# Keys stored once and read in two pieces, SyncE in program order, scales loaded later: a fused attention and feed-forward kernel on one core

## The chip, the core and the metric

The kernel runs on one core of a Trainium2 chip. A core has five engines with queues of their own: TensorE (PE, with its weight loads shown as PEld), VectorE (DVE), ScalarE (ACT), GpSimd (POOL) and SyncE (SP), which here does nothing but issue transfers. 16 DMA engines move data between DRAM and the on-chip memory. Transfers issued by SP are queue q1 of the profile, those of POOL q0, those of ACT q10. The metric is the device time of one execution in microseconds (us); the time of a kernel is the median of its runs.

## The reference

One sequence of 4096 tokens of 256 features goes through causal attention with 16 heads of 16 features, a layer norm, a gated feed-forward network and a second layer norm, all in float32.

```python
xn  = layernorm(x) * gamma + beta
q, k, v = split(xn @ w_qkv.T)                 # 16 heads of 16
sim = causal(q * 16**-0.5 @ k.T)
x   = layernorm(x + softmax(sim) @ v)
h   = silu((x @ w1.T) * s1) * ((x @ w2.T) * s2)     # 1024 wide
h   = gelu((h @ h1.T) * hs1)
h   = gelu((h @ h2.T) * hs2)
out = layernorm(x + (h @ w3.T) * s3)
```

The weights w1, w2, h1, h2 and w3 are small whole numbers (ternary times 8), and each comes with a vector of scales for its outputs.

## The kernel before

**Accuracy by parts.** [...] So Q and K are split into a high part (rounded) and a low part (what is left), and the score is the sum of three products: high by high, high by low, low by high. This is done in one matmul by stacking rows: a K tile has, for each head, 16 rows of high parts, 16 of high parts again, 16 of low parts and 2 rows of ones (KR = 50 rows); a Q tile has 16 rows of high, 16 of low and 16 of high parts, and 2 rows that receive the negated row maximum, itself split in two.

**Blocks and stages.** Tokens are cut into 8 blocks of 512. `projections` (L200 to L293) normalizes a block, transposes it, multiplies it with the weights of K, Q and V, splits K and Q into kh and kl, and stores them in DRAM tensors `kaug`, `qaug` and `vaug`, one of each per block. Per block and per K or Q there are six stores of 256 KB (L269), because the high part is stored twice; in block 0 they go in turn over the queues of ACT, SP and POOL, later all over POOL's. The rows of ones are stored by SP (L274).

**Attention** (`layer`, L296 on) runs 32 steps, one for each block of queries (in the order 0, 1, 2, 3, 4, 6, 7, 5) and each of four groups of 4 heads. Two streams run side by side, and the emission order of the program interleaves them:

- `row_max` (L425 to L473) loads the Q tile qt of the step (two loads of 48 rows, L429), and for each key block up to the query block takes a K tile mk, multiplies (L442), masks the diagonal block (L449) and reduces to row maxima on DVE (L453). At the end the maxima are transposed, negated, split, and written by four small SP transfers (L469, qt<-hl) into the last two rows of qt.
- `scores` (L476 to L498) takes a K tile sk of its own, multiplies again with rows and columns exchanged (L486), and takes the exponential on ACT (L490). `product` (L500) multiplies with the V tile vk into opsum (L504), some units later.

The row-maximum stream runs ahead of the scores by one step and some units. `fetch` (L401 to L421) loads K tiles for both streams: at the start of tile j it issues the load of tile j+1, in two halves (two heads in partitions 0 on, two in partitions 64 on, L410); for sk the V tile follows (L416). mk, sk and vk have two buffers each, qt four. There are 144 mk tiles and 144 sk tiles.

**Feed-forward** (`feed`, from L729) takes a finished block of 512 tokens; its matmuls are dealt out in pieces between the units of attention, so that PE always has work. Its weights are loaded by POOL (L665), 22 tiles of 512 KB for each block. `start` (L675) loads x and the stored attention output `at`, and adds them in `total`. The last block in the order is done by `closing` after attention has ended, and `inspect` (L707) compares the weights with their rounded values on DVE, through mk buffers, near the end.

**Scales.** `scales` (L117) loads four scale vectors in an element by element layout and one broadcast row, and computes w1_half and w12 from them on POOL. It is called in `layer` just before attention begins.

**Order.** PE, DVE, ACT and POOL execute in the order in which the program emits (`in_order`, L63). DMA instructions are left out of that rule, so that a scheduler places them, SP's whole queue among them: it puts the loads of x and of the scales at the front of SP's queue, and loads qt several steps ahead where a buffer is free. An instruction on SP whose buffer or data is not there yet holds up all that stand behind it.

```python
if i.engine in engines and "DMA" not in type(i).__name__:
```

Of the kernel before, what the change touches and what calls it, by code (L numbers as in the profile page):

```python
# [7 lines left out]
F32 = mybir.dt.float32  # L8
FR = mybir.dt.float32r
AF = mybir.ActivationFunctionType  # L10
ALU = mybir.AluOpType
# [4 lines left out]
N, E, H, D = 4096, 256, 16, 16  # L16
# [4 lines left out]
B = 512  # L21
NB = N // B
NQ = H // 4
KR = 50
# [10 lines left out]
ORDER = (0, 1, 2, 3, 4, 6, 7, 5)  # L35
# [12 lines left out]
class Layer:  # L48
# [13 lines left out]
    @contextmanager  # L62
    def in_order(self, *engines):  # L63

        block = self.nc.cur_bb.bb
        start = len(block.instructions)
        yield
        last = {}
        for i in block.instructions[start:]:
            if i.engine in engines and "DMA" not in type(i).__name__:  # L70
                if i.engine in last:
                    self.after(i, last[i.engine])
                last[i.engine] = i.name
# [8 lines left out]
    def run(self):  # L82
        tc, nc, a = self.tc, self.nc, self.a
        with ExitStack() as ctx:
            dram = self.pool(ctx, "dram", space=DRAM)
            cst = self.pool(ctx, "cst")
            self.small = self.pool(ctx, "small", 4)
            self.qaug = [dram.tile([H, 48, B], F32, name=f"qaug{b}") for b in range(NB)]
            self.kaug = [dram.tile([H, KR, B], F32, name=f"kaug{b}") for b in range(NB)]
            self.vaug = [dram.tile([NQ, P, 4, 4, D + 1], F32, name=f"vaug{b}") for b in range(NB)]  # L90
            self.attn = [dram.tile([B, E], F32, name=f"attn{b}") for b in range(NB)]

            self.ident = cst.tile([P, P], F32, name="ident")
            make_identity(nc, self.ident)
            self.mhalf = cst.tile([P, 4], F32, name="mhalf")
            nc.gpsimd.memset(self.mhalf, -0.5)
            self.wbad = cst.tile([P, 22], F32, name="wbad")
            self.wseq = (
                [("glu", g, 0) for g in range(4)]
                + [(n, g, k) for n in ("h1T", "h2T") for g in range(4) for k in range(2)]  # L100
                + [("w3T", 0, k) for k in range(2)]
            )
            self.sc = {}
            for n in ("w1_s", "w2_s", "h1_s", "h2_s"):
                self.sc[n] = cst.tile([P, 8], F32, name=n)
            self.w1_half = cst.tile([P, 8], F32, name="w1_half")
            self.w12 = cst.tile([P, 8], F32, name="w12")
            self.s3 = cst.tile([P, E], F32, name="s3")

            own = mybir.EngineType  # L110
            with ExitStack() as fctx, self.in_order(own.PE, own.DVE, own.Activation, own.Pool):
                self.layer(fctx)
            bad = self.verdict(cst)
            with tc.If(bad > 0), ExitStack() as gctx:
                self.general(gctx)

    def scales(self):  # L117
        for n, t in self.sc.items():
            self.nc.sync.dma_start(t, self.a[n].rearrange("(c p) -> p c", p=P))
        self.nc.gpsimd.tensor_scalar(self.w1_half, self.sc["w1_s"], 0.5, None, ALU.mult)  # L120
        self.nc.gpsimd.tensor_tensor(self.w12, self.w1_half, self.sc["w2_s"], ALU.mult)
        s3 = self.a["w3_s"].rearrange("(o f) -> o f", o=1)
        self.nc.sync.dma_start(self.s3, s3.broadcast_to([P, E]))

# [75 lines left out]
    def projections(self, ctx):  # L200
# [4 lines left out]
        nc, a, ps = self.nc, self.a, self.ps  # L205
# [46 lines left out]
        for b in range(NB):  # L252
            xh, xl = parts.pop(b)
            prods = [(wh, xh, c) for c in range(2)] + [(wl, xh, c) for c in range(2)] + [(wh, xl, c) for c in range(2)]
            for off, dst, order in ((E, self.kaug, (0, 0, 1)), (0, self.qaug, (0, 1, 0))):
                kp = ps.tile([P, 2, B], F32, name="s", tag="s", bufs=3)
                for T in range(2):
                    for n, (wp, xp, c) in enumerate(prods):
                        nc.tensor.matmul(
                            kp[:, T], wp[:, c, off + T * P : off + (T + 1) * P], xp[:, c], start=n == 0, stop=n == 5  # L260
                        )
                kh = wk.tile([P, 2, B], FR, name="kh")
                nc.scalar.copy(kh, kp)
                kl = wk.tile([P, 2, B], FR, name="kl")
                nc.vector.tensor_tensor(kl, kp, kh.bitcast(F32), ALU.subtract)
                for n, (i, g) in enumerate(sorted((i, g) for g, i in enumerate(order))):
                    for T in range(2):
                        queues = (nc.scalar, nc.sync, nc.gpsimd) if b == 0 else (nc.gpsimd,)
                        queues[(2 * n + T) % len(queues)].dma_start(  # L269
                            dst[b][8 * T : 8 * T + 8, 16 * g : 16 * g + 16, :], (kh, kl)[i][:, T].bitcast(F32)  # L270
                        )
                yield 12 * MM, True
                if dst is self.kaug:
                    nc.sync.dma_start(self.kaug[b][:, 48:KR, :], ones)  # L274
                    if b + 1 < NB:
                        yield from front(b + 1, xb)
                        if b + 2 < NB:
                            xb = fetch(b + 2)
            if b + 2 < NB:
                self.layernorm(xb, xb)  # L280
            v = vst[b % 2]
            vps = ps.tile([P, 4, E], F32, name="s", tag="s", bufs=3)
            for t in range(4):
                for n, (wp, xp, c) in enumerate(prods):
                    nc.tensor.matmul(
                        vps[:, t], xp[:, c, t * P : (t + 1) * P], wp[:, c, 2 * E :], start=n == 0, stop=n == 5
                    )
            for t in range(4):
                nc.scalar.copy(v[:, :, t, :, 0:D], vps[:, t].rearrange("p (q h d) -> p q h d", q=NQ, d=D))
            nc.gpsimd.dma_start(  # L290
                self.vaug[b].rearrange("q p t h d -> p q (t h d)"), v.rearrange("p q t h d -> p q (t h d)")
            )
            self.projected = b  # L293
            yield 12 * MM, True

    def layer(self, ctx):  # L296
# [7 lines left out]
        nc = self.nc  # L304
# [65 lines left out]
        half = P // 2  # L370
# [18 lines left out]
        nc.vector.tensor_copy(tri, tri_f)  # L389
        opsum = ps.tile([P, B], F32, name="opsum")  # L390
        nc.vector.memset(opsum, 0.0)
        self.scales()

        steps = [(qb, qd) for qb in ORDER for qd in range(NQ)]
        order = {
# [5 lines left out]
        def fetch(kind, key):  # L401

            seq = order[kind]
            j = seq.index(key)
            while loaded[kind] < min(j + 2, len(seq)) and seq[loaded[kind]][2] <= self.projected:
                qb, qd, kb = nxt = seq[loaded[kind]]
                kt = (mk if kind == "m" else sk).tile([P, 2, B], FR, name=kind + "k")
                for e in range(2):
                    hs = slice(4 * qd + e, 4 * qd + 4, 2)
                    nc.sync.dma_start(  # L410
                        kt[half * e : half * e + KR].bitcast(F32), self.kaug[kb][hs].rearrange("r p t -> p r t")
                    )
                vt = None
                if kind == "s":
                    vt = sk.tile([P, 4, 4, D + 1], F32, name="vk")
                    nc.sync.dma_start(  # L416
                        vt.rearrange("p t h d -> p (t h d)"), self.vaug[kb][qd].rearrange("p t h d -> p (t h d)")
                    )
                tiles[kind, nxt] = kt, vt
                loaded[kind] += 1  # L420
            return tiles[kind, key]  # L421
# [3 lines left out]
        def row_max(qb, qd):  # L425
            qt = qtile[qb, qd] = qp.tile([P, 2, B], FR, name="qt")
            for e in range(2):
                hs = slice(4 * qd + e, 4 * qd + 4, 2)
                nc.sync.dma_start(  # L429
                    qt[half * e : half * e + 48].bitcast(F32), self.qaug[qb][hs].rearrange("r p t -> p r t")  # L430
                )
            mp = small.tile([P, 2, 2, 4, NB], F32, name="mp")
            nc.gpsimd.memset(mp, NEG)
            for kb in range(qb + 1):
# [240 lines left out]
    def start(self, b):  # L675

        nc = self.nc
        self.busy.add("at")
        x1 = self.load(b)
        at = self.fk.tile([P, 4, E], F32, name="at")  # L680
        nc.sync.dma_start(at, tokens(self.attn[b]))

        def total():
            nc.gpsimd.tensor_tensor(x1, x1, at, ALU.add)
            self.free("at")

        self.defer("next", total, 7)
        for delay, step in self.norm_steps(x1, x1):
            self.defer("next", step, delay)
        return x1  # L690
# [383 lines left out]
```

## Time and profile before

| what | value |
|---|---|
| median of 3 runs | 2522.06 us (2519.75 to 2528.87) |
| the profiled execution, its own time | 2522.7 us |
| its span | 2521.0 us |
| mean granted TensorE clock | 0.926 |
| 0 to 240 us: PE busy, DMA share | 163.57 us, 0.69 |
| 240 to 2220 us: PE busy, DMA share | 1876.24 us, 0.47 |
| 2340 to 2521 us: PE busy, DMA share | 107.89 us, 0.34 |
| moved in all | 310.02 MB in 251,811 packets |
| L453, row maxima on DVE | 1152 instructions, 1132 ns each |
| L490, exponentials on ACT | 1152 instructions, 954 ns each |

The first row maximum starts at about 66 us, the last score at 2347 us; before that stretch lies the projection of the first two blocks, after it the last feed-forward block. "DMA share" is the mean busy share of the 16 DMA engines. A row such as "mk<-kaug SPq DMA_DIRECT2D x288, 200.0 KB" says that SP issued 288 transfers of 200 KB from kaug into mk; an mk tile takes two of them. In the waits, "PE s L486 <- DMA qt<-hl: 12.9, 4, 4.7" says that PE's instructions of line 486 waited 12.9 us in all, 4 times, 4.7 us at the longest, until that transfer had landed.

### The profile page before, as it was taken

Reading aid. Unit: us, or ns where it says so; the run is one execution under the profiler, and the core shown is the slowest. Engines: PE = TensorE matmul, PEld = TensorE weight load, DVE = VectorE, ACT = ScalarE, POOL = GpSimd, SP = SyncE. Lnnn points to the kernel's source line nnn. Section 1 sums busy time; section 2 is a strip of 40 time slices with the busy share of each in tenths; the row PEclk is TensorE's granted clock in tenths of the full one; section 3 lists DMA queues with packets and bytes.
Section 4 is the critical chain, followed back from the end, with each engine's and each line's share of the span. In section 5 each row is a group of like instructions: output and inputs, shape, how many; then the busy total and the mean of one; then the engine's idle time right before and its main releaser. Section 6 shows DMA issues by size and latency. Waiting matters only on the chain. (4 is left out here: it accounts for less than half of the span.)

```text
span 2521.0 us, 36370 instructions
## 1 busy us (share of the span) xinstructions
PE 2258.4 (90%) x13986; PEld 1216.5 (48%) x13986; DVE 1563.3 (62%) x1826; ACT 1393.1 (55%) x1698; POOL 705.8 (28%) x1021
## 2 busy tenths in 40 slices
PE   4768999999998999999999999999999999999458
PEld 3545444545454544544455435554455434544246
DVE  3445687675657576676756686666765577662353
ACT  2233555645655666556656655666666676567311
POOL 2333323242313052312404142323204222132201
PEclk8688889979999989999999989998999999999779
DMA  6776834525453544444444535463355343447333
GB/s 189 190 183 160 188 104 112 133 78 125 108 130 98 142 104 116 108 127 119 114 115 120 132 83 134 98 146 93 100 130 140 98 125 89 108 108 197 93 98 85
DMA packets 251811, 310.02 MB, mean 123 GB/s; under 512 B 41328, under 2 KB 179696, under 8 KB 251632
## 3 DMA queue, kind: packets, MB, share of 16 engines
q1 hardware_dynamic: 141920, 184.87, 26.2%
q0 software_dynamic: 108352, 120.91, 21.8%
q8 instruction: 113, 1.85, 0.3%
q10 hardware_dynamic: 1360, 1.84, 0.2%
q14 instruction: 66, 0.54, 0.1%
HBM read 268.45 MB, written 38.54 MB: 122 GB/s over the span
## 5 line engine op out<-in xcount | busy, mean ns | idle before, releaser
L453 DVE TENSOR_REDUCE mp<-s 128x2 f32<-128x1024 f32 (+3 forms) x1152 | 1265.0, 1132 | 562.8 <-PE s L442 406.1
L490 ACT ACTIVATE p<-s 128x1024 f32<-128x1024 f32 (+3 forms) x1152 | 1062.2, 954 | 672.2 <-PE s L486 658.9
L486 PE MATMUL s<-qt,sk 50*128 50x512 f32 (+3 forms) x2304 | 513.5, 452 | 85.0 <-DVE mp L453 49.5
L442 PE MATMUL s<-mk,qt 48*128 48x512 f32 (+3 forms) x2304 | 512.2, 446 | 55.5 <-DVE mp L453 19.3
L504 PE MATMUL opsum<-p,vk 128*17 128x512 f32 (+3 forms) x4608 | 558.0, 586 | 1.2 <-POOL p L493 1.0
L823 PE MATMUL m<-act,wt 128*128 128x512 f32 x1792 | 477.2, 409 | 0.7 <-DVE xl L778 0.7
L486 PEld LDWEIGHTS s<-qt,sk 50*128 50x128 f32 x2304 | 222.1, 192 | 398.9 <-DVE mp L453 145.2
L823 PEld LDWEIGHTS m<-act,wt 128*128 128x128 f32 x1792 | 321.9, 189 | 123.7 <-issue 53.0
L442 PEld LDWEIGHTS s<-mk,qt 48*128 48x128 f32 x2304 | 229.0, 196 | 305.0 <-ACT p L490 134.0
L504 PEld LDWEIGHTS opsum<-p,vk 128*17 128x17 f32 x4608 | 97.6, 98 | 232.9 <-issue 213.2
L493 POOL TENSOR_SCALAR_AFFINE_SELECT p<-p 128x256 f32<-128x256 f32 x256 | 102.2, 409 | 293.9 <-ACT p L490 292.9
L665 POOL DMA_DIRECT2D wt<-h1T_in x64 | 48.9, 764 | 425.0 <-PE m L823 230.9
L665 POOL DMA_DIRECT2D wt<-h2T_in x64 | 48.6, 759 | 366.5 <-PE m L823 311.5
L748 POOL TENSOR_TENSOR act<-raw,act 128x512 fp32r<-128x512 f32 x112 | 143.0, 1277 | 8.9
L831 ACT ACTIVATE raw<-m,h_s 128x512 f32<-128x512 f32 x112 | 77.1, 688 | 107.6 <-PE m L823 107.6
L795 PE MATMUL m<-xh,wt 128*128 128x512 f32 x224 | 104.9, 468 | 12.4 <-DVE th L799 9.5
L449 PEld LDWEIGHTS s<-tri,pick 64*128 64x128 f32 x1024 | 96.5, 205 | 8.1 <-DVE tri L389 1.2
L795 PE MATMUL m<-xl,wt 128*128 128x512 f32 x224 | 92.4, 413 | 0.0
L449 PE MATMUL s<-tri,pick 64*128 64x128 f32 (+1 forms) x1024 | 88.6, 252 | 1.0 <-DVE tri L389 1.0
L747 POOL CAST act<-raw 128x512 fp32r<-128x512 f32 x112 | 68.2, 609 | 42.4 <-ACT raw L752 42.4
L747 POOL CAST act<-th 128x512 fp32r<-128x512 f32 x56 | 34.4, 614 | 144.9 <-DVE th L801 144.6
L748 POOL TENSOR_TENSOR act<-th,act 128x512 fp32r<-128x512 f32 x56 | 71.5, 1277 | 4.7
(126 smaller groups left out, 1496.3 us busy)
## 6 DMA issues: line engine op xcount, KB each, us to landing
mk<-kaug SPq DMA_DIRECT2D x288, 200.0 KB
sk<-kaug SPq DMA_DIRECT2D x288, 200.0 KB
wt<-h1T_in POOLq DMA_DIRECT2D x64, 512.0 KB, 4.2
wt<-h2T_in POOLq DMA_DIRECT2D x64, 512.0 KB, 4.1
vk<-vaug SPq DMA_DIRECT2D x144, 136.0 KB
qt<-qaug SPq DMA_DIRECT2D x64, 192.0 KB
wt<-w1T_in POOLq DMA_DIRECT2D x34, 256.0 KB, 3.8
wt<-w2T_in POOLq DMA_DIRECT2D x34, 256.0 KB, 5.1
```

The costliest lines, as they stand in the source:

```text
L442: nc.tensor.matmul(m[:, e, :k1], qt[rows, r, t * P : (t + 1) * P], kt[rows, r, :k1], start=True, stop=kb != qb,)
L449: nc.tensor.matmul(m[:, e, k1 - P + half * i : k1], pick[rows, i], tri[rows, : P - half * i], start=False, stop=i == 1,)
L453: nc.vector.tensor_reduce(mp[:, r, :, t, kb], m[:, :, :k1], AX.X, ALU.max)
L486: nc.tensor.matmul(s[:, e, lo:], kt[rows, r, t * P : (t + 1) * P], qt[rows, r, lo:], start=True, stop=True)
L490: nc.scalar.activation(p[:, :, lo:], s[:, :, lo:], AF.Exp, scale=0.25)
L493: nc.gpsimd.affine_select(out=p[:, :, lo : lo + P], in_=p[:, :, lo : lo + P], compare_op=ALU.is_ge, fill=0.0, base=0, pattern=[[0, 2], [1, ...
L504: nc.tensor.matmul(opsum[32 * j : 32 * j + D + 1, lo:], vt[:, t, j], pt[j // 2][:, j % 2, lo:], start=first, stop=last,)
L665: self.nc.gpsimd.dma_start(dst, src)
L747: nc.gpsimd.tensor_copy(hi, src)
L748: nc.gpsimd.tensor_tensor(lo, src, hi.bitcast(F32), ALU.subtract)
L795: nc.tensor.matmul(s, wt[:, 2 * i + k, cols], x[:, k], start=k == n == 0, stop=k == n == 1)
L823: nc.tensor.matmul(s, wts[k // 4][:, k % 4, cols], x[:, k % 4], start=k == n == 0, stop=k == 7 and n == 1)
```

## The change

Three edits are made together.

1. `kaug` is stored as 16 high rows, 16 low rows and 2 rows of ones (34 rows for each head instead of 50), `qaug` as 16 high and 16 low rows (32 instead of 48). The stores per block and tensor fall from six to four. The tiles in on-chip memory are unchanged. Each half of a K tile is now loaded in two pieces: 16 rows (the high part) and then 34 rows (high, low, ones); each half of a Q tile as 32 rows and then 16 rows. A new method `rows` issues one piece.
2. SP's instructions, DMA instructions included, are put under the rule of program order.
3. `scales` is called at the first `start`, and w1_half and w12 are computed in that block's `total`.

```diff
-            if i.engine in engines and "DMA" not in type(i).__name__:
+            if i.engine in engines and (i.engine == mybir.EngineType.SP or "DMA" not in type(i).__name__):
...
-            self.qaug = [dram.tile([H, 48, B], F32, name=f"qaug{b}") for b in range(NB)]
-            self.kaug = [dram.tile([H, KR, B], F32, name=f"kaug{b}") for b in range(NB)]
+            self.qaug = [dram.tile([H, 32, B], F32, name=f"qaug{b}") for b in range(NB)]
+            self.kaug = [dram.tile([H, 34, B], F32, name=f"kaug{b}") for b in range(NB)]
...
-            with ExitStack() as fctx, self.in_order(own.PE, own.DVE, own.Activation, own.Pool):
+            with ExitStack() as fctx, self.in_order(own.PE, own.DVE, own.Activation, own.Pool, own.SP):
...
+    def rows(self, dst, first, src):
+        n = src.shape[1]
+        self.nc.sync.dma_start(dst[first : first + n].bitcast(F32), src.rearrange("r p t -> p r t"))
...
-                for n, (i, g) in enumerate(sorted((i, g) for g, i in enumerate(order))):
+                for i, part in enumerate((kh, kl)):
                     for T in range(2):
...
-                            dst[b][8 * T : 8 * T + 8, 16 * g : 16 * g + 16, :], (kh, kl)[i][:, T].bitcast(F32)
+                            dst[b][8 * T : 8 * T + 8, 16 * i : 16 * i + 16, :], part[:, T].bitcast(F32)
...
-                    nc.sync.dma_start(self.kaug[b][:, 48:KR, :], ones)
+                    nc.sync.dma_start(self.kaug[b][:, 32:34, :], ones)
...
-        self.scales()
...
                 for e in range(2):
                     hs = slice(4 * qd + e, 4 * qd + 4, 2)
-                    nc.sync.dma_start(
-                        kt[half * e : half * e + KR].bitcast(F32), self.kaug[kb][hs].rearrange("r p t -> p r t")
-                    )
+                    self.rows(kt, half * e, self.kaug[kb][hs, 0:16])
+                    self.rows(kt, half * e + 16, self.kaug[kb][hs])
...
-                nc.sync.dma_start(
-                    qt[half * e : half * e + 48].bitcast(F32), self.qaug[qb][hs].rearrange("r p t -> p r t")
-                )
+                self.rows(qt, half * e, self.qaug[qb][hs])
+                self.rows(qt, half * e + 32, self.qaug[qb][hs, 0:16])
...
         self.busy.add("at")
+        if b == ORDER[0]:
+            self.scales()
         x1 = self.load(b)
...
             self.free("at")
+            if b == ORDER[0]:
+                nc.gpsimd.tensor_scalar(self.w1_half, self.sc["w1_s"], 0.5, None, ALU.mult)
+                nc.gpsimd.tensor_tensor(self.w12, self.w1_half, self.sc["w2_s"], ALU.mult)
```

The order of the instructions on PE is the same in both kernels. SP issues 640 transfers more for K and Q tiles.

More of the change, by code (lines that the diff above doesn't have):

```diff
@@ L119, in scales @@
             self.nc.sync.dma_start(t, self.a[n].rearrange("(c p) -> p c", p=P))
-        self.nc.gpsimd.tensor_scalar(self.w1_half, self.sc["w1_s"], 0.5, None, ALU.mult)
-        self.nc.gpsimd.tensor_tensor(self.w12, self.w1_half, self.sc["w2_s"], ALU.mult)
         s3 = self.a["w3_s"].rearrange("(o f) -> o f", o=1)
@@ L254, in projections @@
             prods = [(wh, xh, c) for c in range(2)] + [(wl, xh, c) for c in range(2)] + [(wh, xl, c) for c in range(2)]
-            for off, dst, order in ((E, self.kaug, (0, 0, 1)), (0, self.qaug, (0, 1, 0))):
+            for off, dst in ((E, self.kaug), (0, self.qaug)):
                 kp = ps.tile([P, 2, B], F32, name="s", tag="s", bufs=3)
@@ L265, in projections @@
                 nc.vector.tensor_tensor(kl, kp, kh.bitcast(F32), ALU.subtract)
-                for n, (i, g) in enumerate(sorted((i, g) for g, i in enumerate(order))):
+                for i, part in enumerate((kh, kl)):
                     for T in range(2):
                         queues = (nc.scalar, nc.sync, nc.gpsimd) if b == 0 else (nc.gpsimd,)
-                        queues[(2 * n + T) % len(queues)].dma_start(
-                            dst[b][8 * T : 8 * T + 8, 16 * g : 16 * g + 16, :], (kh, kl)[i][:, T].bitcast(F32)
+                        queues[(2 * i + T) % len(queues)].dma_start(
+                            dst[b][8 * T : 8 * T + 8, 16 * i : 16 * i + 16, :], part[:, T].bitcast(F32)
                         )
```

## The prediction

> **What bounds the kernel now.** I read the page's busy shares and slices first, then who PE waits for, then the DMA parts, and last single stretches.
>
> ```profile
> PE 2258.4 (90%) x13986; PEld 1216.5 (48%) x13986; DVE 1563.3 (62%) x1826; ACT 1393.1 (55%) x1698; POOL 705.8 (28%) x1021
> ...
> PE   4768999999998999999999999999999999999458
> ...
> DMA  6776834525453544444444535463355343447333
> ```
>
> PE is at nine tenths from slice 5 to slice 37 and the DMA engines are on average half idle there. PE is the bound of the long middle; the first four slices and the last three are not full.
>
> ```profile
> PE s L486 <- DVE mp L453: 49.5, 88, 3.2
> ...
> PE s L486 <- DMA qt<-hl: 12.9, 4, 4.7
> ...
> PE s L442 <- DMA qt<-qaug: 0.5, 1, 0.5
> ...
> PE s L486 <- DMA vk<-vaug: 0.3, 1, 0.3
> ```
>
> These are PE's waits (total us, times, longest). Transfers cost PE almost nothing, and no row at all shows PE waiting for mk or sk, the K tiles. So today each K tile is early; the question is whether it stays so.
>
> ```profile
> q1 hardware_dynamic: 141920, 184.87, 26.2%
> q0 software_dynamic: 108352, 120.91, 21.8%
> ...
> mk<-kaug SPq DMA_DIRECT2D x288, 200.0 KB
> sk<-kaug SPq DMA_DIRECT2D x288, 200.0 KB
> ...
> vk<-vaug SPq DMA_DIRECT2D x144, 136.0 KB
> qt<-qaug SPq DMA_DIRECT2D x64, 192.0 KB
> ```
>
> K tiles are most of SP's queue (q1): 576 transfers of 50 rows x 2 heads, 100 packets of 2 KB each. The next view shows how wide such a transfer runs (last three columns: granted clock, DMA share, GB/s).
>
> ```profile
> 4.00:5.00 1.00, 0.00 (x0) 0.00 (x0) 0.00 (x0) 0.00 (x0) 0.00 (x0) 1.00 1.08 424
> 1615.60:1615.90 0.30, 0.10 (x2) 0.10 (x2) 0.30 (x2) 0.30 (x1) 0.30 (x1) 1.00 0.65 253
> 1615.50:1616.50 1.00, 0.70 (x6) 0.32 (x10) 1.00 (x2) 1.00 (x2) 0.92 (x2) 1.00 0.63 219
> ```
>
> At 4 us the 128-row loads of x fill all 16 engines (share 1.08, 424 GB/s). At 1615.6 us, where the last issues were the two halves of one mk tile (at 1614.08), the share stands at 0.65 and 0.63, which is 10 of 16 (0.625). A 50-row transfer runs on 10 engines, not 16. 253 GB/s over 10 engines is 81 ns for a packet of 2 KB; the longer window, with the change from one half to the other in it, gives 94 ns, so a transfer costs about 0.13 us beside its 10 packets an engine.
>
> The packet count says the same for all of them. Adding up the full list of DMA issues (rows times issues, by size) gives 130,176 data packets on q1; 141,920 - 130,176 = 11,744 are left for 1016 transfers. One closing packet per engine fits exactly if the 576 K transfers use 10 engines, the 132 with 8 rows outermost (qt<-hl and the four 8x16x512 stores of block 0) use 8, and the other 308 use 16: 5760 + 1056 + 4928 = 11,744. So 50 gives 10, 8 gives 8, 48 and 128 give 16: each time the largest divisor up to 16.
>
> **The change, part by part.**
>
> (1) K in two pieces. Each half of a K tile becomes a load of 16 rows and one of 34 rows. Bytes are the same (16 + 34 = 50). 16 rows go on 16 engines, 2 packets each: nothing. 34 has the divisors 1, 2, 17, 34. By the pattern above that is 2 engines with 34 packets each. The trace has no such transfer, so both ends: on 16 engines (at most 6 packets, 0.5 us) the edit costs nothing; on 2 engines it takes 34 x 0.081 + 0.13 = 2.9 us, and the second half follows on the same two engines (at 1615 us the two halves also shared ten). I take 2, the divisor, because three sizes fit it to the packet.
>
> [...]
>
> Per K tile the two engines then work 2 x (2.9 + 2 x 0.081 + 0.13) = 6.4 us, against about 1.9 us (2 x 0.94) on ten engines now. They also carry their share of everything else: q0's 21.8% and, of q1's 26.2%, the 36% of bytes that are not K tiles (118 of 184.87 MB are), together 31% of the time. So a tile takes 6.4 x 1.31 = 8.3 us; with 0.9 us to the first packet and 0.3 us to the signal it lands 9.5 us after issue if alone, and up to 17.8 us if the other kind's tile stands in front.
>
> How much time is there? From the timeline's SP rows to the first L442 or L486 matmul of the tile: mk 11.2 us (5% of tiles), 13.3 (quarter), 15.9 (median); sk 10.6, 13.1, 15.2. A tile of each kind is used every 15.3 us (mk) and 15.7 us (sk), with two buffers: a load can start only when the tile before the last is done. Lateness summed over all 144 mk and 144 sk tiles, for a landing time L: 3 + 5 us at L = 10, 17 + 23 at 12, 76 + 89 at 14, 192 + 223 at 16, 273 + 320 at 17. Averaged over L from 9.5 to 17.8 this is 101 + 120 = 221 us; the other kind is in service 8.3 of 15.5 us, about half the time, so 110 us. Nothing hides it: PE runs in the order of the program and waits.
>
> Ends: with no sharing (5.8 us a tile, L from 7 to 13) lateness is about 10 us; by plain throughput, 288 x 6.4 = 1843 us plus 31% of 2521 = 782 us is 2625 us of work in the 2282 us from the first K load (43.8) to the last (2326), which is 340 us too much.
>
> (2) SP in program order. qt is now loaded far ahead of its first reader (5 us in the first step, over 50 us in 25 of the 32). In the new order a step's four qt loads stand behind the pieces of the step's first mk tile, and often behind sk and vk of the other stream; vk waits for the last product before it (358.9 us in 116 waits on SP, longest 9.2), and mk, qt and the row maxima queue behind it. qt's first reader is that step's first matmul. So qt lands with or after K work that takes 0 to 8.3 us on the two engines: 32 steps by 3.5 us = 112 us; ends 32 x 1 and 32 x 8. Issues themselves are cheap: 640 more at 0.34 us (0.67 for two in the timeline) is 218 us of a queue that stands idle most of the time.
>
> (3) Fewer stores. 32 of POOL's stores of 256 KB go: 8.4 MB, 37 us at the 225 GB/s of that stage, and 19 us of POOL issue (0.6 each) that nobody waits for. One PE gap is clearly theirs: 12.2 us before 65.6 us, with a DMA share of 0.81. I take -12; ends 0 and -37.
>
> (4) Scales. Five loads (8.1 us of SP issue at the start now: 3.61 + 3.96 + 0.58) move to the first feed-forward block, ahead of x, at, one step's row maxima and an sk tile, whose leads are 8 to 15 us: +2, ends 0 and 8. The two POOL operations (0.5 us) move along and are covered until the first tanh.
>
> Sum: 2522.7 (profiled execution; span 2521.0, median 2522.06) + 110 + 112 - 12 + 2 = 2735 us.
>
> **Rivals.**
> Spread wide: a 34-row load uses 8 or more engines. For it: the bytes are equal, and 34 is an extrapolation. Against: 50 rows did not get 16. A tile then costs 2 us, leads of 11 us hold for qt too, and what remains is the stores' -12 to -37 and +2 for the scales: 2488 to 2513, say 2500 us, faster. It decides from 8 engines on (9 packets, 0.9 us).
> Only the queue: K spreads well enough, but qt comes just in time: 32 x 1 to 32 x 2 us, less 10 for the rest: 2545 to 2577, say 2560 us. Against: SP is idle most of the time.
> Saturated: the mean recorded packet holds (26.2% of 16 x 2521 us over 184.87 MB is 117 ns per 2 KB): 576 x 36 x 0.117 = 2426 us + 782 = 3208 in 2282 us, +926 less what other engines catch up, about 3250 us. Against: 81 ns is shown, and two engines do not compete with eight more of their kind.
>
> **How the numbers follow.** Forecast 0.72, wide 0.10, only the queue 0.08, saturated 0.10. The forecast's own range is 2587 (+10 lateness, 32 x 2 for qt, -10 for the rest) to 2965 (+340 throughput, +112 qt, -10). The range 2545 to 3000 takes in most of the queue rival and leaves the wide and the saturated ones out. A measurement of this kernel tells 0.5% (13 us) from nothing: faster 0.09 (nearly all of wide), same 0.04, slower 0.87.
>
> **What would show it.** Right: PE rows waiting for DMA mk, sk and qt<-qaug of tens of us each; a DMA share near 0.12 (2 of 16) in quiet stretches where a 34-row load runs; PE below 90% through the middle slices; lower granted clock behind the gaps (0.66 at 53 to 65 us today); q1 packets = data plus 2 for each 34-row load. Wrong: shares near 0.6 or 1 there, or K waits absent. If only qt appears, step (2) was right and (1) was not.

## The result and the profile after

The changed kernel takes 2914.16 us (median of 4 runs, 2908.55 to 2925.62) against 2523.72 us for the kernel before beside it (4 runs): a ratio of 1.155, 95% interval 1.151 to 1.159. It is slower by 390 us; the forecast was 2735 us, slower by 212.

The page of the changed kernel, its busy shares, slices, queues and DMA issues:

```profile
PE 2388.6 (82%) x13986; PEld 1280.0 (44%) x13986; DVE 1571.4 (54%) x1826; ACT 1395.7 (48%) x1698; POOL 691.8 (24%) x991
...
PE   5667677988888888998899888888899888999738
...
PEclk8778788978989989989899899899899888998869
...
DMA  4445323434434443434244433443344332344533
...
q1 hardware_dynamic: 147280, 184.37, 21.3%
q0 software_dynamic: 104032, 113.03, 18.5%
...
mk<-kaug SPq DMA_DIRECT2D x288, 136.0 KB
sk<-kaug SPq DMA_DIRECT2D x288, 136.0 KB
```

PE executes the same 13,986 matmuls, but its slices stand at 8 where nine was the rule before, and the DMA engines are busy a smaller share of the time (21.3% and 18.5%, before 26.2% and 21.8%). So the 16 engines together had bandwidth left; PE is kept waiting by transfers that use little of it. The sum of PE's time shows two parts. The span grew by 389.5 us (2521.0 to 2910.5). PE's busy time grew by 130.2 us (2258.4 to 2388.6) for the same work, so its idle time grew by the other 259.3. PE's waits, largest of those for transfers (total us, times, longest):

```profile
PE s L442 <- DMA qt<-qaug: 166.7, 30, 12.2
...
PE s L486 <- DMA sk<-kaug: 69.2, 28, 7.5
...
PE s L442 <- DMA mk<-kaug: 56.9, 24, 5.4
```

With two more rows of 5.3 and 0.9 us these come to 299 us, against 13.7 us in the kernel before: 285 us more, while PE's waits for other engines shrank by 26. Stretches of 1 us, which showed ten engines before, now show two. In a quiet stretch of the changed kernel (columns: window, length, busy time of PE, PEld, DVE, ACT and POOL, then granted clock, DMA share, GB/s):

```profile
1610.00:1611.00 1.00, 0.08 (x1) 0.00 (x0) 0.00 (x0) 0.39 (x1) 0.00 (x0) 0.90 0.17 61
...
1616.00:1617.00 1.00, 1.00 (x4) 0.56 (x2) 0.00 (x0) 0.00 (x0) 0.00 (x0) 0.50 0.13 49
1617.00:1618.00 1.00, 1.00 (x5) 0.62 (x6) 0.01 (x1) 0.58 (x1) 0.00 (x0) 0.68 0.13 49
1618.00:1619.00 1.00, 1.00 (x12) 0.25 (x12) 1.00 (x1) 0.83 (x2) 0.00 (x0) 1.00 0.13 49
```

A share of 0.13 is 2 of 16 engines (0.125). 49 GB/s over two engines is 84 ns for a packet of 2 KB, close to the 81 ns that the prediction took from the ten-engine loads. From 1605 to 1621 us the share never falls below this, so the two engines are working off a backlog. The sk tile whose second half PE waits for until 1612.88 us (the line of PE's timeline stands in the last section; each tile has 16 matmuls of L486, so their count tells which tile it is) had been issued 16 us before:

```profile
1595.44 1.34 SPq L120 DMA_DIRECT2D sk<-kaug  x4
```

The queue's packets agree: data are 256 packets fewer than before (SP has two stores of block 0 less), 129,920; 147,280 - 129,920 = 17,360 closing packets. The 16-row pieces, qt, qt<-hl, the stores and the rest take 9216 + 2048 + 1024 + 16 + 3904 = 16,208 of them; 1152 are left for the 576 loads of 34 rows, exactly two each.

How the qt loads fare in program order, in a view of SP's timeline (start, length, what was issued, how often):

```profile
1185.07 1.45 SPq L120 DMA_DIRECT2D mk<-kaug  x4
1186.63 2.34 SPq L120 DMA_DIRECT2D qt<-qaug  x4
```

and PE's timeline of the same kernel, where the bracket holds the idle time before the instruction:

```profile
1198.31 1.65 PE L442 MATMUL s<-mk,qt 48*128 48x512 f32 x2 [3.18 <-DMA qt<-qaug]
```

qt is issued right behind an mk tile, and PE gets it over 9 us after its last issue, although by the count above its own pieces of 32 and 16 rows have 16 closing packets each, so all 16 engines take part. While PE waits, two engines' worth of work is all that goes on:

```profile
1196.00:1197.00 1.00, 0.00 (x0) 0.00 (x0) 0.00 (x0) 0.00 (x0) 0.00 (x0) 1.00 0.15 46
```

This fits two engines that still have 34-row pieces in front of qt's share; the trace does not name the engine of a packet.

### The profile page after: what moved, and what is told of

It reads as the page before. It is cut to its first block, busy times and chain, and to the rows that moved or that the text cites. A ratio compares the mean times of both kernels' runs of the same rounds, so it can differ in the third digit from the quotient of the medians.

```text
span 2910.5 us, 37196 instructions
## 1 busy us (share of the span) xinstructions
PE 2388.6 (82%) x13986; PEld 1280.0 (44%) x13986; DVE 1571.4 (54%) x1826; ACT 1395.7 (48%) x1698; POOL 691.8 (24%) x991
## 3 DMA queue, kind: packets, MB, share of 16 engines
q1 hardware_dynamic: 147280, 184.37, 21.3%
q0 software_dynamic: 104032, 113.03, 18.5%
## 4 chain that ended last, share of the span: by engine, by line
PE 48%; DMA 31%; DVE 10%; ACT 4%; SPq 4%; issue 2%; POOL 1%; ACTq 0%; POOLq 0%; DVEq 0%
PE opsum L504 12%; PE m L828 11%; DMA sk<-kaug 9%; DMA mk<-kaug 9%; DMA qt<-qaug 8%; PE s L442 8%; PE s L486 8%; DVE mp L453 6%; PE m L800 3%; SPq L120 3%; ACT p L490 2%; PE bank L929 2%; PE m L855 1%; PE s L262 1%; DMA xb<-x_in 1%
## 5 line engine op out<-in xcount | busy, mean ns | idle before, releaser
L442 PE MATMUL s<-mk,qt 48*128 48x512 f32 (+3 forms) x2304 | 563.5, 464 | 267.9 <-DMA qt<-qaug 166.7
L486 PE MATMUL s<-qt,sk 50*128 50x512 f32 (+3 forms) x2304 | 552.9, 464 | 124.8 <-DMA sk<-kaug 69.2
L504 PE MATMUL opsum<-p,vk 128*17 128x512 f32 (+3 forms) x4608 | 585.2, 612 | 1.3 <-POOL p L493 1.1
L828 PE MATMUL m<-act,wt 128*128 128x512 f32 x1792 | 506.1, 427 | 0.7 <-DVE xl L783 0.7
L442 PEld LDWEIGHTS s<-mk,qt 48*128 48x128 f32 x2304 | 255.8, 205 | 546.3 <-issue 301.3
L486 PEld LDWEIGHTS s<-qt,sk 50*128 50x128 f32 x2304 | 242.6, 200 | 447.9 <-issue 201.1
L828 PEld LDWEIGHTS m<-act,wt 128*128 128x128 f32 x1792 | 340.5, 200 | 135.0 <-issue 59.9
L855 PE MATMUL m<-wt,act 128*128 128x256 f32 x448 | 69.4, 316 | 5.2 <-DVE th L862 5.2
```

The costliest lines, as they stand in the source:

```text
L442: nc.tensor.matmul(m[:, e, :k1], qt[rows, r, t * P : (t + 1) * P], kt[rows, r, :k1], start=True, stop=kb != qb,)
L486: nc.tensor.matmul(s[:, e, lo:], kt[rows, r, t * P : (t + 1) * P], qt[rows, r, lo:], start=True, stop=True)
L504: nc.tensor.matmul(opsum[32 * j : 32 * j + D + 1, lo:], vt[:, t, j], pt[j // 2][:, j % 2, lo:], start=first, stop=last,)
L828: nc.tensor.matmul(s, wts[k // 4][:, k % 4, cols], x[:, k % 4], start=k == n == 0, stop=k == 7 and n == 1)
L855: nc.tensor.matmul(yp[:, t], x[:, k % 4, q : q + P], wts[k // 4][:, k % 4], start=k == n == 0, stop=k == 7 and n == 1,)
```

## The experiments

They are called e1 to e9 below. Rows added to `kaug` fill partitions that no matmul reads. "Before" in each comparison was run beside the kernel, on the same chip. The waits of 137 us for K and 174 us for qt that the expectations give for the changed kernel count those of the weight loads (PEld) too; PE's own are 127 and 167.

**1. 36 rows in place of 34** (36 has the divisor 12):

```diff
-            self.kaug = [dram.tile([H, 34, B], F32, name=f"kaug{b}") for b in range(NB)]
+            self.kaug = [dram.tile([H, 36, B], F32, name=f"kaug{b}") for b in range(NB)]
...
-        ones = one.tile([32, B], F32, name="ones")
+        ones = one.tile([64, B], F32, name="ones")
...
-                    nc.sync.dma_start(self.kaug[b][:, 32:34, :], ones)
+                    nc.sync.dma_start(self.kaug[b][:, 32:36, :], ones)
```

> The changed kernel with 36 rows for each head in kaug instead of 34 (four rows of ones instead of two, two of them not used by any matmul), so each half of a K tile reads two rows more. Theory (34 rows have 2 as their largest divisor up to 16 and run on two DMA engines; 36 have 12): a lower piece is 6 packets an engine, a K tile about 2 us of the busiest engine instead of 6.4; PE's waits for mk and sk (137 us in the changed kernel) fall under 5 us, those for qt (174 us) under 30, time 2500 to 2550 us, in spite of 4% more bytes in K tiles. Rival (the 640 transfers more, or SP's program order, cause the loss, whatever the number of rows): waits stay and the time stays over 2800 us.

Measured: 2591.5 us against 2517.6, ratio 1.027 (1.024 to 1.030). PE's waits in this kernel:

```profile
PE s L442 <- DMA qt<-qaug: 46.4, 19, 8.6
...
PE s L442 <- DMA mk<-kaug: 10.3, 3, 4.9
```

3% more bytes on SP's queue (189.64 MB in place of 184.37) and 317 us less (74 us above its kernel before, where the change is 390 above): the count of DMA engines is the cause of most of the loss. Its queue holds 155,600 packets, of which 132,480 are data; less the same 16,208 there remain 6912 closing packets for 576 loads, twelve each. But 2500 to 2550 us was expected; 74 us remain, and waits for qt lead them (46 us, where under 30 was expected; those for K are 22 in place of under 5).

**2. 37 rows, a prime**: the same edit with 37 and a ones tile of 80 rows.

> The same with 37 rows, which is one row more than the run before and a prime. Theory: one engine, 74 packets, 6.0 us a lower piece, a K tile at least 12.5 us on that engine; 288 tiles are 3600 us of one engine, and with its share of all else (about 700 us) the time is 4100 to 4600 us. Rival (the engine count does not follow the divisor): between 2500 and 2950 us, like its neighbours.

Measured in one run: 4637.5 us, 37 us beyond the upper end of what was expected, with PE busy 59% of the span at a mean granted clock of 0.724. Its longest waits:

```profile
PE s L442 <- DMA mk<-kaug: 585.8, 101, 20.4
PE s L486 <- DMA sk<-kaug: 550.9, 106, 16.0
```

One row more than the last kernel and 2046 us longer. By the same count its queue has 576 closing packets for 576 loads, one each. Bytes cannot explain the order 36 (2591), 34 (2914), 37 (4637); the largest divisor up to 16 (12, 2, 1) does.

**3. The order alone**: the kernel before, with only SP put in program order.

```diff
-            if i.engine in engines and "DMA" not in type(i).__name__:
+            if i.engine in engines and (i.engine == mybir.EngineType.SP or "DMA" not in type(i).__name__):
...
-            with ExitStack() as fctx, self.in_order(own.PE, own.DVE, own.Activation, own.Pool):
+            with ExitStack() as fctx, self.in_order(own.PE, own.DVE, own.Activation, own.Pool, own.SP):
```

> The kernel before with SP's transfers in program order alone: 50-row loads, six stores, early scales. Theory (the order is harmless while a K tile takes 2 us on ten engines; qt comes later but in time): PE waits for qt under 40 us, none for mk or sk, 2515 to 2570 us. Rival (the order alone puts qt behind vk's wait and costs most of the 392 us): over 2700 us.

Measured: 2601.1 us against 2517.6, ratio 1.033 (1.030 to 1.036), more than expected. Two rows of its waits:

```profile
PE s L442 <- DMA qt<-qaug: 27.9, 11, 10.3
PE m L219 <- ACT xb L146: 26.4, 2, 14.6
```

The order costs 83 us with wide K loads too. Against the expectation there is also one wait for sk, of 8.8 us. PE runs the same instructions in the same order in all these kernels, so their starts can be compared one by one: this kernel is 45 us behind the kernel before at 417 us and 75 us at 2087 us. Over half of the loss falls in the first 420 us, where a step has few tiles to cover its qt, and the loads of x stand behind stores in SP's queue (the third one is issued at 31.6 us, in the kernel before at 16.3). How much each of the two costs was not measured.

**4. The change without the order**: 34 rows, scales late, SP placed by the scheduler.

```diff
-            with ExitStack() as fctx, self.in_order(own.PE, own.DVE, own.Activation, own.Pool, own.SP):
+            with ExitStack() as fctx, self.in_order(own.PE, own.DVE, own.Activation, own.Pool):
```

> The changed kernel with SP's queue left to the scheduler again: 34-row pieces, four stores, late scales. Theory: the two engines stay the narrow place, so PE waits for mk and sk stay at 100 to 250 us, but qt is loaded ahead again and its waits (174 us) fall under 30; 2700 to 2850 us. Rival 1 (the order is the cause): about 2530 us. Rival 2 (the two engines cost all of it and qt's waits only move to mk and sk): 2880 us or more.

Measured: 2807.5 us against 2517.6, ratio 1.115 (1.113 to 1.118). Its waits:

```profile
PE s L442 <- DMA mk<-kaug: 67.9, 35, 4.3
PE s L486 <- DMA sk<-kaug: 66.8, 30, 5.1
PE s L442 <- DMA qt<-qaug: 60.0, 12, 10.7
```

The time is as expected: 290 us above its kernel before, so some 100 of the change's 390 go with the order. That qt's waits would fall under 30 us was wrong. The four longest (8.0 to 10.7 us) stand in steps whose last qt piece SP issues only 5 to 9 us before the step's first matmul starts; with 36 rows (e5) the first matmul of these steps starts 2 to 5 us after that issue, so qt also lands later behind narrow loads. The scheduler does not load qt as early here as in the kernel before: over 50 us ahead in 14 of the 32 steps, where it was 25.

**5. 36 rows and no order**: the first and the fourth edit together. What is left of the change is the fewer stores and the late scales.

> 36 rows in kaug and SP's queue left to the scheduler: the change without its two-engine loads and without its order; what is left of it are the fewer stores, the two pieces and the scales. Theory (both losses are taken away, 32 stores of 256 KB fewer free the first 240 us): PE waits for mk and sk under 10 us in all, for qt under 15; 2500 to 2518 us, that is 0 to 18 us below the kernel before. Rival (640 more transfers cost by themselves): 2530 us or more.

Measured: 2519.8 us against 2518.8, ratio 1.000 (0.998 to 1.002). The whole loss of 390 us is undone by these two edits. The expected gain of up to 18 us from the stores was missing from the end, but not from the beginning: by PE's instructions the kernel is 16 us ahead at 257 us and level again at 417. A window of it in between:

```profile
327.00:375.00 48.00, 42.72 (x261) 21.91 (x259) 31.81 (x38) 20.30 (x28) 11.28 (x19) 0.71 0.36 94
```

and PE's timeline in that window:

```profile
338.79 0.76 PE L442 MATMUL s<-mk,qt 48*128 48x512 f32 x1 [3.00 <-DMA qt<-qaug]
```

PE is busy 42.7 of 48 us and gets only 261 matmuls done, at a granted clock of 0.71, around a wait of 3.0 us for qt. But the clock is at half before that wait, and also before the one of 1.35 us that ends at 298.53 us, with PE busy all the time:

```profile
280.10:297.00 16.90, 16.89 (x96) 9.12 (x88) 8.68 (x12) 8.46 (x12) 1.77 (x5) 0.50 0.28 77
...
324.50:335.70 11.20, 11.20 (x82) 7.45 (x74) 6.95 (x9) 3.39 (x5) 1.36 (x4) 0.50 0.26 75
```

Whether the waits for qt or the clock by itself ate the gain was open, and experiment 8 was made for it.

**6. 36 rows, the order, and qt loaded one step earlier.** The loads of qt become a function that `row_max` calls for its own step, where they are still missing, and then for the next.

```diff
-        def row_max(qb, qd):
+        def queries(qb, qd):
+            if (qb, qd) in qtile or qb > self.projected:
+                return
             qt = qtile[qb, qd] = qp.tile([P, 2, B], FR, name="qt")
...
+        def row_max(qb, qd):
+            queries(qb, qd)
+            qt = qtile[qb, qd]
+            i = steps.index((qb, qd)) + 1
+            if i < len(steps):
+                queries(*steps[i])
```

> 36 rows and program order (2591 us as it stood), with the four loads of a qt issued at the start of the row maxima of the step before, one step earlier in the program. Theory (after the first blocks the order costs through qt alone, 46 us of waits in 19 steps): waits for qt under 10 us, 2540 to 2560 us; what remains above the kernel before stems from the first 300 us, where loads of x stand behind stores. Rival (the order costs through the queue as a whole, so waits only move): 2575 us or more.

Measured: 2530.5 us against 2518.8, ratio 1.004 (1.002 to 1.006); no wait for qt<-qaug is left on PE. Of the 74 us of experiment 1 this takes 62, better than expected. Not all of the 62 belongs to the program order: without the order the same edit gains some 20 us as well (experiment 8).

**7. 34 rows, the order, and qt ahead**: the changed kernel with the edit of experiment 6 alone.

> The changed kernel (34 rows, program order) with the same early qt loads. Theory (two engines too full: qt's waits were partly those of the K tiles in front of it): of 174 us of qt waits under 25 are left, mk and sk waits rise from 137 to 150 to 230 us; 2780 to 2850 us, close to the run without order (2807). Rival (qt's waits and K's are independent): 2914 less 170, 2745 us or less.

Measured: 2803.0 us against 2518.8, ratio 1.112 (1.108 to 1.116). Its waits:

```profile
PE s L451 <- DMA mk<-kaug: 112.7, 49, 10.9
...
PE s L495 <- DMA sk<-kaug: 76.3, 31, 11.8
...
PE s L451 <- DMA qt<-qaug: 4.0, 2, 2.1
```

(L451 and L495 are L442 and L486, moved by the inserted lines.) This is as expected: with qt out of the way the kernel is still 284 us above its kernel before, and the waits for K grow from 127 to 189 us, which fits a PE that now arrives earlier.

**8. 36 rows, no order, qt ahead**: experiment 5 with the edit of 6.

> 36 rows, the scheduler's order of SP, and the qt loads emitted one step earlier. The question is whether the fewer stores are worth anything in the end. Theory A (36 rows, no order, without this edit: 2519.8 us against 2518.8; its profile was 16 us ahead at 257 us and level again at 417 us, where its granted clock stood at 0.80 and 0.71 against 0.95 and 0.88 in two stretches): what is gained early is lost again to the clock, so it ends within 8 us of the kernel before, 2511 to 2527, although the 12.6 + 9.4 us of waits for qt are gone. Theory B: the waits for qt alone gave the 16 us back, so without them it ends 10 to 20 us below the kernel before, 2498 to 2509.

Measured: 2501.7 us against 2520.3, ratio 0.992 (0.990 to 0.995): theory B. In the same stretch as in experiment 5 this kernel shows

```profile
327.00:375.00 48.00, 42.62 (x276) 20.87 (x274) 39.14 (x51) 27.46 (x36) 18.60 (x25) 0.96 0.46 111
```

The busy time is equal, but 276 matmuls are done in it in place of 261, at a clock of 0.96. It is 20 us ahead of the kernel before at 336 us and stays so to the end (22 us at 2346 us). So the late loads of qt are what took the gain back in experiment 5, since nothing else differs. By which way is less clear. Of the 15 us that were lost there after 257 us, waits for qt are 5.1 (the longest of its five, 7.5 us, lies earlier), and the two longest stretches of half clock had begun before the waits in them. So it is not shown that the waits brought on the slow clock. The 20 us are the gain of all that is left of the change, with qt ahead; the prediction's term for the fewer stores lies near it, but no run takes the stores alone. This is the one version that beats both kernels.

Experiments 6 and 8 differ only in the order, and each against its own kernel before they are 30 us apart (12 and -19). So the order costs 30 us even when qt is loaded ahead, and 73 when it is not (e1 against e5).

**9. 36 rows, the order, qt ahead, and the scales put back** to the start of attention: experiment 6 with the third part of the change undone.

```diff
         nc.vector.memset(opsum, 0.0)
+        self.scales()
...
-        if b == ORDER[0]:
-            self.scales()
```

> 36 rows, SP in the order of the program, qt ahead, and the scales put back at the start of attention, so that nothing is left of that part of the change. Theory A (in order, the scales stand ahead of a qt and an sk tile at the first feed-forward block: one gap of 5.0 us there): 3 to 8 us below the same kernel with the scales late (2530.5), so 2522 to 2528. Theory B (8 us of issue at the start of attention stall the queue in the same way, since there it stands ahead of the first K tiles): no gain, 2528 to 2536.

Measured: 2522.3 us against 2520.3, ratio 1.000 (0.998 to 1.002). That is 8 us less than experiment 6, at the edge of what theory A expected (10 us, if each is taken against its own kernel before). Experiments 6 and 9 were not timed in one comparison, and their intervals against the kernel before overlap a little (1.0017 to 1.0062 and 0.9981 to 1.0023), so a cost is likely rather than shown, and its size is uncertain.

| kernel | rows of kaug | SP in order | qt ahead | time, us | above its kernel before, us | ratio to before (interval) |
|---|---|---|---|---|---|---|
| e2 | 37 | yes | no | 4637.5 (one run) | 2120 | 1.842 (one run) |
| the change | 34 | yes | no | 2914.2 | 390 | 1.155 (1.151 to 1.159) |
| e4 | 34 | no | no | 2807.5 | 290 | 1.115 (1.113 to 1.118) |
| e7 | 34 | yes | yes | 2803.0 | 284 | 1.112 (1.108 to 1.116) |
| e3 (stores, scales as before) | 50 | yes | no | 2601.1 | 83 | 1.033 (1.030 to 1.036) |
| e1 | 36 | yes | no | 2591.5 | 74 | 1.027 (1.024 to 1.030) |
| e6 | 36 | yes | yes | 2530.5 | 12 | 1.004 (1.002 to 1.006) |
| e9 (scales as before) | 36 | yes | yes | 2522.3 | 2 | 1.000 (0.998 to 1.002) |
| e5 | 36 | no | no | 2519.8 | 1 | 1.000 (0.998 to 1.002) |
| e8 | 36 | no | yes | 2501.7 | -19 | 0.992 (0.990 to 0.995) |

## Why the prediction was right, and where its sum was too small

The direction and the mechanisms were right, and the time lies inside the range; the likeliest time was 179 us too low. By its steps:

**Two engines for 34 rows: right**, to the packet, with 84 ns a packet. This rules out "spread wide" (the share is 0.13, not 0.5 and more). "Saturated" fell by its time, which was 336 us above the measured one; its 117 ns a packet did not hold in the quiet stretch, though over the whole queue the mean is still 110 (21.3% of 16 x 2910.5 us over 184.37 MB). "Only the queue" fell too: with qt out of the way (e7) PE still waits 189 us for K tiles. The pattern that the packets of the kernel before gave, the largest divisor up to 16, held for the three sizes tried: 1152, 6912 and 576 closing packets for 576 loads of 34, 36 and 37 rows, that is 2, 12 and 1 engines.

**K tiles late, +110: mis-sized.** This is the step that failed. Each against the same kernel with 36 rows, the narrow loads cost 289 us (e4 against e5), 272 (e7 against e6) or 317 (the change against e1). Two things in the step were too small. First, the prediction found 221 us of lateness with the two engines shared between mk and sk, and then halved it, because the other kind is in service about half the time. In e7, where hardly any other transfer is waited for, PE's waits for K are 189 us: nearer to the 221 before halving. (Of the small terms, the 0.9 us to the first packet and the 0.3 us to the signal are 0.88 and 0.64 us in the trace of the kernel before, for the two halves of mk issued at 1614.08 us.) Second, the sum added up waits only. PE is busy 128 us more in e7 (2386.5 against 2258.4) for the same matmuls, at a mean granted clock of 0.881 in place of 0.926. The prediction named the lower clock as a sign to look for, but gave it no price. The profiled execution of e7 adds up so: 128 us of busy time, 184 of waits for transfers (K and the few others, less the 13.7 of before), and 25 less of other idle time (23 of it waits for other engines), make the 287 us by which its span (2808.0) is longer.

**qt just in time, +112: near in size, in part by luck.** Each against its own kernel before, the order costs 100 us on top of the narrow loads (390 against 290), and loading qt a step ahead gets 106 us back (390 against 284). But the 112 were 32 waits of 3.5 us and nothing for the clock. PE's waits for qt are 167 us in 30 waits, 5.6 us each, and in part they stand in the place of K waits, which are 127 us where e4 has 135 and e7 189; these errors go opposite ways. With wide K loads the order still costs 73 to 83 us (e1 against e5, and e3), where the rival that spoke of this case had 32 to 64.

**Stores, -12 to -37: not shown by itself.** The gain of about 20 us in e8 lies in its range, with the other parts of the change and qt ahead in it, and it shows as nothing when a few qt loads are late (e5). Of the 32 stores that go, 30 were POOL's and two SP's.

**Scales, +2 (0 to 8):** some 8 to 10 us by e6 and e9, at the upper end or above it, with the doubt given there.

**The signs** named all appeared: PE rows for mk, sk and qt of tens of us each, a share near 0.12 in quiet stretches (0.13), PE below 90% through the middle, the lower clock (0.873 in the mean, before 0.926), two closing packets a load.

## What to carry to other kernels

Count the rows of a transfer before its bytes: on this queue 34 rows ran on 2 DMA engines, 37 on one and 36 on twelve (by the closing packets of a load), and two rows of padding were worth over 270 us in each pairing here (390 to 74, 290 to 1, 284 to 12). Price a wait of TensorE at more than its length: here eight matmuls behind one of 2.8 us took 3.78 us where 2.11 was shown before it, at a granted clock of 0.50, and PE's busy time grew by 130 us beside the 285 us of longer waits for transfers. And when a queue is put in program order, emit each load where its lead is long enough, because the scheduler that had moved it ahead no longer does: loading qt one step earlier got back 106 us with narrow loads and 62 with 36 rows.

## What the runs showed that was not expected

**Eight matmuls behind a wait of 2.8 us took 1.7 us longer.** PE's timeline of the changed kernel in the stretch of windows shown above:

```profile
1603.92 2.11 PE L828 MATMUL m<-act,wt 128*128 128x512 f32 x8
...
1609.61 0.47 PE L486 MATMUL s<-qt,sk 50*128 50x512 f32 x1 [1.02 <-ACT x L149]
1612.88 0.79 PE L486 MATMUL s<-qt,sk 50*128 50x512 f32 x1 [2.81 <-DMA sk<-kaug]
1613.60 3.78 PE L828 MATMUL m<-act,wt 128*128 128x512 f32 x8
```

The same eight matmuls of L828 take 2.11 us before the gap and 3.78 us after it. The windows give 0.90 for 1610 to 1611, 0.50 after it and 0.68 for 1617 to 1618. In windows of 0.1 us the granted clock is 1.00 up to 1610.8 us, 0.53 in the next, 0.50 from 1610.9 to 1617.6 us, 0.83 in the next and 1.00 from 1617.7 us on. So it was half for 6.8 us in all, beside idle times of 1.0 and 2.8 us; it fell 0.7 us after the second of them had begun. That the idle times brought this on is not shown. Of the 198 windows of 10 us between 240 and 2220 us, 17 stand below a clock of 0.8 in the kernel before and 48 in the changed one.

**A few late loads hid a gain of 0.8%.** e5 and e8 differ only in when qt is loaded; the first measures as unchanged and the second is 0.8% faster. The five waits of matmuls for qt in e5, 12.6 us in all, are less than the 19 us between the two; the rest goes with the lower clock (0.71 against 0.96 in the window shown), whose cause is open.

**Scale loads by element were slow to issue, and in order they held up SP's queue.** In e1, at the first feed-forward block, each scale vector of 4 KB takes SP about 2 us to issue, where a vk tile of 136 KB takes 0.35 us (at 279.92 us), in this view of SP's timeline:

```profile
258.98 4.04 SPq L124 DMA_DIRECT2D w_s<-w_s_in  x2
263.07 4.12 SPq L124 DMA_DIRECT2D h_s<-h_s_in  x2
...
269.33 2.71 SPq L469 DMA_DIRECT2D qt<-hl  x4
272.14 7.69 SPq L120 DMA_DIRECT2D sk<-kaug  x4
```

The last parts of qt and the next sk tile are issued behind them, and L486 waits for transfers 1.1 us at 281.6 and 4.6 us at 286.7 us.
